# A written-out issue order for a two-layer graph network: scores and weighted sums on TensorE's row and column tiles, grouped differently

## The chip, the cores and the metric

One core of one Trainium2 chip runs the kernel. The metric is the device time of one execution in microseconds (us). TensorE (PE in the profile, PEld for its weight loads), VectorE (DVE), ScalarE (ACT) and GpSimd (POOL) each take their instructions in the order in which the program holds them; SyncE (SP) issues the DMA transfers. An instruction that depends on another engine waits on a semaphore, and everything queued behind it on its own engine waits too.

## The reference, cut to what matters

There are 64 graphs of 256 nodes with 256 features. Each goes through two layers; weights are shared by all graphs. All data are f32, `adj` is int32 (here 0 or 1). Head width is 32, and there are 8 heads.

```python
# layer 0
q = src @ Wq + bq; k = src @ Wk + bk                       # 8 heads of 32
attn = softmax(q @ k.T / sqrt(32))
out = sum over r of (attn * (adj == r)) @ (src @ Wv[r] + bv[r])
x = layernorm(src + out @ Wo + bo)
x = layernorm(x + gelu(x @ W1 + b1) @ W2 + b2)             # 1024 hidden
# layer 1
q, k, v = x @ Wq, x @ Wk, x @ Wv
e = q @ k.T; e = where(e >= 0, e, 0.2 * e)
h = softmax(where(adj > 0, e, -9e15)) @ v
y = layernorm(concat(layernorm(h), x) @ Wffn.T) + x
```

## The kernel before, in words

Everything of one graph is some 120 steps, written in the function `fast_path` as calls of `op(engine, reads, writes, emit)`. A step belongs to one engine and issues one to sixteen instructions. The 64 graphs overlap, like iterations of a software pipeline, and the order in which the steps of all graphs stand is written out by hand: `STARTS` gives each step of a graph a start, graph g is set off by `g * PERIOD`, and `in_order` sorts all steps of all graphs by that number. For the first four and the last four graphs a list of its own per graph (`FIRST`, `LAST`) takes the place of `STARTS`. The numbers serve as sort keys alone; nothing in the program waits for a time. Within an engine the sorted order is the order of execution.

```python
def in_order(programs, starts, period, first, last):
    ops = []
    for g, p in enumerate(programs):
        edge = first[g] if g < len(first) else last[g - len(programs)] if g >= len(programs) - len(last) else None
        at = edge or [starts[o.name] for o in p]
        ops += [(round(g * period + t, 3), o) for t, o in zip(at, p)]
    return [o for _, o in sorted(ops, key=lambda x: x[0])]
```

The names that follow are the keys of `STARTS`, in which the first digit is the layer, the second one is the group of four heads (hg 0 or 1), and `/0`, `/1` are the two pairs of heads of that group. `#2` and `#3` are the second and third step that write a tile.

- `pq0`, `pk0`, `pq1`, `pk1`, `pv1`, `pwo`, `pwa`, `pwb` are linear maps on TensorE, each four f32 matmuls of 128x128 weights by 256 columns (the trace shows two records for each, so x8); `pva0`, `pva1` are the two halves of layer 0's values; `py0`, `py1`, `ph` are transposes; `ph0`, `ph2`, `ph4`, `ph6` and `pw2` to `pw2#8` are the feed-forward part (32 + 32 records). All of these use the whole 128x128 array.
- `s00`, `s01`, `s10`, `s11` are the scores of four heads (`score`, L434). A head has only 32 rows to contract, so four heads lie beside one another on four row tiles (32x128) of the array; x16 records.
- `po00`, `po01`, `po10`, `po11` are the weighted sums (`weighted`, L470) and the row sums of the softmax (L475). A head has 32 output columns, so four heads lie on four column tiles (128x32). Layer 0 has parts `e`, `m` and `es` (x16, x16, x8 records), layer 1 has `e` and `es`.
- The scores of a group go to one PSUM tile `s` with room for one group alone (`TAGS`: "s" has one buffer), which is read pair by pair by two engines. In layer 0 ACT makes `e00/0` and `e00/1` of it (exp, L448) and DVE makes `m00/0` and `m00/1` (mask added, L457; ACT's exp `m00/0#2` follows in place). In layer 1 DVE makes `e10/0` and `e10/1` (mask added, L457) and ACT makes `m10/0` and `m10/1` (scaled relu, L706); POOL adds the two (`e10/0#2`, L710), and ACT takes the exp (`e10/0#3`). `es` is the sum of two halves on POOL (L501).
- `rd00` is DVE's reciprocal of the row sums (L484), `o0/0` and `o0/1` are the two products `po * rd` of layer 0 (L487), and `DVE:po00` is a check of the sums (L492). `pwo` multiplies by `o0/0` in its first matmul and by `o0/1` in its second one.
- `mv0` to `mv3` are the statistics of the four layer norms on DVE, `rs0` to `rs3` POOL's inverse roots, `y0`, `y1`, `y2` the normalised tiles; `q1`, `k1`, `v1`, `y0T`, `y1T` and `hT` are ACT's copies out of PSUM.

All tiles but `s` rotate through two to four buffers; PSUM's other tiles share one pool of four buffers ("g").

Of the kernel before, what the change touches and what calls it, by code (L numbers as in the profile page):

```python
# [44 lines left out]
def in_order(programs, starts, period, first, last):  # L45
# [4 lines left out]
    for g, p in enumerate(programs):  # L50
# [50 lines left out]
    "xT": 16.39, "x": 17.62, "pk0": 18.03, "adj": 19.67, "neg": 20.08, "pq0": 21.31, "k0": 22.13, "q0": 25.00,  # L101
    "s00": 31.15, "m00/1": 33.61, "e00/0": 37.30, "e00/1": 38.52, "m00/1#2": 39.34, "m00/0": 40.16, "s01": 40.57,
    "e01/0": 40.98, "e01/1": 41.39, "m00/0#2": 44.26, "pva0": 45.49, "es01/1": 46.31, "v0/0": 46.72, "pva1": 47.13,
    "v0/1": 48.36, "es00/0": 48.77, "es00/1": 50.82, "m01/0": 52.05, "m01/0#2": 52.87, "m01/1": 54.92,
    "es01/0": 55.33, "m01/1#2": 57.38, "po00": 57.79, "rd00": 58.20, "po01": 58.61, "o0/0": 60.25,
    "DVE:po01": 61.48, "rd01": 62.30, "o0/1": 62.70, "pwo": 63.11, "DVE:po00": 63.52, "res": 64.34, "pwo#2": 65.57,
    "mv0": 66.80, "rs0": 67.21, "y0": 69.26, "py0": 71.72, "y0T": 72.54, "ph6": 75.41, "ph0": 76.64, "hT/6": 77.87,
    "ph2": 78.69, "hT/2": 79.10, "ph4": 79.51, "hT/0": 79.92, "hT/4": 80.74, "pw2": 81.97, "pw2#2": 82.38,
    "r1": 82.79, "r1#2": 83.20, "pw2#3": 84.43, "pw2#4": 84.84, "pw2#5": 85.66, "pw2#6": 86.07, "pw2#7": 86.48,
    "pw2#8": 88.93, "pw2#9": 91.80, "mv1": 93.03, "rs1": 93.44, "y1": 94.67, "py1": 97.54, "y1T": 97.95,  # L110
    "pk1": 100.00, "ACT:adj": 100.41, "pq1": 104.10, "q1": 104.51, "k1": 109.02, "s10": 109.43, "m10/0": 109.84,
    "pv1": 110.66, "v1": 111.07, "x2": 111.89, "pwb": 113.93, "e10/0": 114.75, "e10/1": 115.16, "e10/0#2": 115.98,
    "m10/1": 118.44, "e10/1#2": 118.85, "e10/0#3": 120.49, "es10/0": 120.90, "zb": 122.95, "s11": 123.36,
    "e11/1": 123.77, "x2#2": 124.18, "e11/0": 124.59, "e10/1#3": 125.82, "es10/1": 126.23, "m11/0": 127.05,
    "m11/1": 127.46, "e11/1#2": 128.28, "e11/0#2": 130.33, "po10": 131.56, "rd10": 134.02, "o1/0": 135.25,
    "e11/1#3": 136.89, "e11/0#3": 137.70, "es11/0": 138.11, "es11/1": 139.75, "po11": 142.21, "DVE:po10": 142.62,
    "rd11": 143.85, "o1/1": 145.08, "DVE:po11": 145.90, "ph": 149.18, "pwa": 149.59, "mv2": 151.23, "rs2": 151.64,
    "pwa#2": 152.46, "mv3": 153.28, "rs3": 153.69, "y2": 155.74, "y2#2": 156.15, "y2#3": 156.56, "SP:y2": 156.97,
# [3 lines left out]
        -2847.053, -2618.669, -2552.639, -2604.994, -2706.544, -2524.281, -2429.355, -2491.963, -2326.15, -2291.878,  # L122
        -2205.017, -2453.681, -2501.433, -2475.116, -1979.242, -2495.418, -2281.166, -2149.469, -1954.32, -1950.672,
        -2629.93, -2490.837, -2900.007, -2402.608, -1755.256, -2397.873, -2429.046, -2408.233, -2387.015, -2337.739,
        -2248.383, -2096.592, -2381.743, -2040.963, -2323.494, -1986.344, -2170.731, -2048.634, -1860.558, -2191.888,
        -2201.038, -2121.273, -1987.509, -1858.163, -1687.597, -1539.069, -1758.675, -1901.191, -1868.775, -1849.204,
        -1797.723, -1842.922, -1866.564, -1901.189, -1864.039, -1710.05, -1635.372, -1608.525, -1601.055, -1611.923,
        -1504.663, -1503.313, -1503.311, -1454.211, -1453.749, -1428.651, -1397.418, -1365.689, -1263.132, -1333.428,
        -1307.057, -1302.867, -1269.069, -1279.736, -1246.049, -1318.829, -1287.58, -1268.965, -1234.872, -1196.915,
        -1176.186, -1166.684, -1155.815, -1135.153, -1127.66, -1127.658, -1125.664, -1116.163, -1109.387, -1096.892,  # L130
        -1068.525, -1058.771, -834.708, -1034.909, -1034.369, -1037.42, -971.802, -873.683, -861.526, -817.316,
        -794.117, -948.046, -931.884, -938.676, -839.591, -800.872, -786.885, -935.815, -938.986, -873.329, -822.37,
        -800.254, -703.594, -628.579, -521.145, -703.592, -852.402, -753.92, -797.646, -753.918, -687.087, -549.142,
        -801.786, -794.56, -679.67, -651.382, -613.255, -519.88, -503.788, -460.172, -508.16, -452.842, -406.466,
        -405.026, -445.465, -387.29, -386.804, -373.855, -368.241, -277.528, -258.371, -211.016,
    ],
    [
        -1712.66, -1443.453, -1558.578, -1409.383, -424.973, -1332.342, -1515.918, -1376.199, -1389.201, -1376.896,
        -1176.315, -1175.399, -1171.179, -1142.744, -1372.605, -1177.435, -1233.494, -1225.381, -1169.756, -1364.499,
        -1211.174, -1210.635, -1283.409, -1142.483, -1107.236, -1024.81, -1042.32, -1168.101, -1163.006, -1109.044,  # L140
        -1086.417, -1040.287, -1117.876, -1135.775, -1092.749, -1107.742, -1028.857, -1019.047, -1019.045, -962.29,
        -953.415, -933.383, -905.03, -894.712, -878.269, -878.267, -878.265, -878.267, -829.154, -849.496, -805.626,
        -860.667, -839.105, -834.236, -762.88, -849.583, -795.469, -753.483, -652.438, -623.714, -612.52, -604.112,
        -604.11, -604.108, -597.853, -597.851, -580.455, -541.025, -525.23, -510.162, -510.16, -234.294, 26.726,
        -461.818, -418.06, -444.927, -353.251, -347.025, -276.942, -284.894, -256.944, -353.249, -292.158, -353.247,
        -288.969, -272.27, -239.253, -352.105, -312.477, -253.791, -237.655, -177.565, -140.907, -63.211, -56.41,
        -132.185, -252.617, -248.041, -236.522, -133.806, -99.059, -66.449, -235.239, -211.498, -143.046, -63.735,
        -23.871, -15.497, 7.986, 8.437, -15.495, 28.391, 37.806, 44.002, 37.535, 66.321, 66.323, 87.244, 87.246,
        116.225, 189.089, 204.842,
    ],  # L150
    [
        -1229.881, -526.973, -1181.68, -1178.71, 66.635, -396.146, -1031.055, -966.68, -943.117, -935.039, -608.969,
        -560.147, -579.485, -523.949, -808.47, -704.853, -753.672, -752.036, -617.846, -650.977, -671.842, -631.081,
        -641.14, -494.019, -442.274, -439.507, -456.199, -629.154, -609.944, -493.554, -466.947, -559.795, -577.488,
        -482.336, -418.455, -494.253, -414.141, -410.734, -406.722, -370.63, -396.854, -333.908, -310.914, -309.856,
        -309.854, -305.407, -305.13, -200.379, -114.553, -302.188, -284.917, -285.604, -156.698, -263.97, -217.918,
        -280.388, -230.946, -154.247, -111.16, -83.43, -79.414, -74.774, -71.445, -70.202, -70.114, -67.694, -67.692,
        -67.69, -53.693, -53.691, -53.689, -24.507, 209.443, 29.562, 64.838, -35.526, 9.223, 71.488, 99.662, 113.468,
        120.616, 69.818, 89.502, 70.022, 89.536, 110.394, 124.527, 109.105, 79.783, 120.842, 123.12, 124.465, 131.394,
        133.646, 137.555, 133.656, 123.327, 128.611, 127.875, 129.152, 133.924, 133.926, 123.329, 127.217, 128.709,  # L160
        133.424, 138.627, 142.388, 142.522, 146.364, 145.361, 151.44, 151.442, 153.783, 152.66, 153.785, 153.787,
        155.037, 155.83, 196.784, 209.445, 209.447,
    ],
    [
        -394.579, -455.288, -369.201, -318.002, -85.508, -1.925, -382.842, -372.891, -372.581, -353.322, -106.738,
        -80.656, -102.13, -71.463, -265.115, -179.435, -120.231, -102.022, -128.718, -168.609, -153.486, -32.837,
        -58.709, -10.119, 11.78, 27.092, 37.379, -119.809, -73.356, -86.43, -39.705, -50.805, -93.331, -55.921,
        -14.902, -55.763, 4.094, 33.398, 33.4, 47.121, 58.796, 65.314, 65.316, 67.626, 72.399, 72.484, 72.486, 72.401,
        78.893, 74.741, 81.291, 76.79, 81.396, 75.033, 81.051, 79.917, 81.961, 83.124, 83.126, 84.564, 85.156, 88.277,
# [898 lines left out]
```

## Time and profile before

| | us |
|---|---|
| median of 3 runs | 2936.52 |
| lowest and highest | 2935.5, 2936.69 |
| the profiled execution's own time | 2934.98 |
| its span in the profile | 2932.8 |
| PE busy in the span | 2882.9 (98%) |
| PE's granted clock, mean | 0.995 |
| DVE, ACT, POOL busy | 1961.4 (67%), 1788.6 (61%), 2017.2 (69%) |

The profiled execution took 2.2 us more than its span, and 1.5 us less than the median of the runs. Times in the timeline are microseconds from the start of the span: the first column is the start of a group of like instructions, the second one is its length up to the end of the last of them. As matmuls overlap, what a group costs TensorE is read as the distance from its start to the start of the next group. A remark in brackets at the end of a line is idle time of that engine before the group, and who ended it.

### The profile page before, as it was taken

How to read it: one execution, taken by the hardware profiler on the slowest of the kernel's cores; microseconds unless marked ns; L12 is line 12 of the kernel's file. 1: busy time of each engine (PE TensorE's matmuls, PEld its weight loads, DVE VectorE, ACT ScalarE, POOL GpSimd, SP SyncE). 2: the span in 40 equal slices, each digit the busy share in tenths (PEclk: the TensorE clock that was granted, in tenths of full speed). 3: DMA queues.
4: the chain of work that ended last, by engine and by line, in shares of the span. 5: the costliest groups of instructions: out<-in, count | busy, mean ns of one | idle time of the engine just before them, and what ended most of it. 6: DMA issues, size and time to landing. Idle time of an engine off the chain costs nothing.

```text
span 2932.8 us, 53746 instructions
## 1 busy us (share of the span) xinstructions
PE 2882.9 (98%) x21770; PEld 2154.7 (73%) x21770; DVE 1961.4 (67%) x3668; ACT 1788.6 (61%) x3009; POOL 2017.2 (69%) x1542
## 2 busy tenths in 40 slices
PE   7999999999999999999999999999999999999996
PEld 5777777777777777777777777777777777777774
DVE  4676676676766766766767667667667676676674
ACT  4656656566566566566665665665666656656653
POOL 2657767767767667677667676676776676766666
PEclk9999999999999999999999999999999999999997
DMA  3000100000000000000000000000000000010000
GB/s 123 15 19 16 33 30 15 30 19 26 30 15 30 30 15 30 30 15 30 21 24 30 16 30 30 16 30 30 15 30 23 23 30 16 30 34 15 30 16 8
DMA packets 74331, 76.65 MB, mean 26 GB/s; under 512 B 4448, under 2 KB 73568, under 8 KB 74080
## 3 DMA queue, kind: packets, MB, share of 16 engines
q1 hardware_dynamic: 74080, 73.17, 7.8%
q8 instruction: 174, 2.85, 0.4%
q14 instruction: 77, 0.63, 0.1%
HBM read 56.37 MB, written 16.78 MB: 25 GB/s over the span
## 4 chain that ended last, share of the span: by engine, by line
PE 96%; DVE 1%; POOL 1%; ACT 1%; issue 1%; DMA 0%; SPq 0%; DVEq 0%; ACTq 0%; POOLq 0%
PE ph L658 15%; PE pw L676 15%; PE po L470 12%; PE s L434 9%; PE pva L610 8%; PE pq L338 8%; PE pk L338 7%; PE pv L352 4%; PE pwa L352 4%; PE po L475 4%; PE pwo L352 4%; PE pwb L352 4%; PE py L364 2%; PE ph L364 1%; POOL e L710 1%
## 5 line engine op out<-in xcount | busy, mean ns | idle before, releaser
L710 POOL TENSOR_TENSOR e<-e,m 128x1024 f32<-128x1024 f32 x256 | 601.3, 2359 | 231.7 <-DVE e L457 148.8
L501 POOL TENSOR_TENSOR es<-e 128x512 f32<-128x512 f32 x512 | 644.4, 1274 | 153.1 <-ACT e L448 143.1
L457 DVE TENSOR_TENSOR m<-s,neg 128x1024 f32<-128x1024 f32 x256 | 311.8, 1219 | 483.8 <-PE s L434 327.7
L484 DVE RECIPROCAL rd<-po 128x256 f32<-128x256 f32 x256 | 449.2, 1755 | 132.1 <-PE po L475 124.5
L410 POOL TENSOR_TENSOR rs<-ve,neg_half 128x2 f32<-128x2 f32 x256 | 178.5, 697 | 479.6 <-DVE ve L405 479.3
L706 ACT ACTIVATE m<-s 128x1024 f32<-128x1024 f32 x256 | 255.2, 1022 | 371.2 <-PE s L434 226.1
L658 PE MATMUL ph<-y0T,w 128*128 128x256 f32 x2048 | 459.2, 382 | 0.7 <-ACT y0T L380 0.7
L676 PE MATMUL pw<-w,hT 128*128 128x256 f32 x2048 | 459.0, 382 | 0.0
L676 PEld LDWEIGHTS pw<-w,hT 128*128 128x128 f32 x2048 | 383.9, 190 | 75.6 <-issue 25.1
L658 PEld LDWEIGHTS ph<-y0T,w 128*128 128x128 f32 x2048 | 383.8, 190 | 71.2 <-issue 20.6
L457 DVE TENSOR_TENSOR e<-s,neg 128x1024 f32<-128x1024 f32 x256 | 302.1, 1218 | 146.8 <-PE s L434 122.9
L448 ACT ACTIVATE e<-s 128x1024 f32<-128x1024 f32 x256 | 258.9, 1014 | 187.4 <-PE s L434 167.1
L448 ACT ACTIVATE m<-m 128x1024 f32<-128x1024 f32 x256 | 269.5, 1055 | 66.8 <-DVE m L457 66.8
L434 PE MATMUL s<-q,k 32*128 32x256 f32 x4096 | 293.3, 400 | 3.1 <-DVE e L457 1.4
L448 ACT ACTIVATE e<-e 128x1024 f32<-128x1024 f32 x256 | 270.4, 1056 | 27.1 <-POOL e L710 26.2
L470 PE MATMUL po<-e,v 128*32 128x256 f32 x4096 | 276.4, 385 | 4.3 <-ACT e L448 4.3
L434 PEld LDWEIGHTS s<-q,k 32*128 32x128 f32 x4096 | 185.1, 184 | 89.9 <-issue 78.7
L610 PE MATMUL pva<-wv,xT 128*128 128x512 f32 x512 | 237.0, 605 | 0.0
L470 PEld LDWEIGHTS po<-e,v 128*32 128x32 f32 x4096 | 114.1, 109 | 125.5 <-issue 45.4
L665 ACT ACTIVATE hT<-ph,cols 128x256 f32<-128x256 f32 x512 | 194.6, 488 | 3.4 <-PE ph L658 2.6
L610 PEld LDWEIGHTS pva<-wv,xT 128*128 128x128 f32 x512 | 92.1, 189 | 115.7 <-issue 115.4
L475 PE MATMUL po<-es,ones 128*32 128x256 f32 x2048 | 160.2, 381 | 4.0 <-POOL es L501 4.0
(90 smaller groups left out, 4546.5 us busy)
## 6 DMA issues: line engine op xcount, KB each, us to landing
adj<-adjT_dram SPq DMA_DIRECT2D x64, 256.0 KB, 3.6
xT<-xT_dram SPq DMA_DIRECT2D x64, 256.0 KB, 3.0
x<-x_dram SPq DMA_DIRECT2D x64, 256.0 KB, 3.1
out_dram<-y SPq DMA_DIRECT2D x64, 256.0 KB, 2.2
w<-L_gnn_W_dram SPq DMA_DIRECT2D x2, 1024.0 KB, 10.3
rows<-rows_dram SPq DMA_DIRECT2D x1, 896.0 KB, 7.4
wv<-L_gnn_Wv_dram SPq DMA_DIRECT2D x3, 256.0 KB, 7.2
wq<-L_gnn_Wq_dram SPq DMA_DIRECT2D x2, 256.0 KB, 5.9
```

The source lines that it names most:

```text
L338: nc.tensor.matmul(pt[:, o, :], lhsT=w[:, c, o * P : (o + 1) * P], rhs=s[:, c, :], start=(c == 0), stop=(c == KC - 1),)
L352: nc.tensor.matmul(pt[:, t, :], lhsT=T(s)[:, c, t * P : (t + 1) * P], rhs=w, start=(n == 0), stop=(n == len(parts) - 1),)
L434: nc.tensor.matmul(s[:, j, c, :], lhsT=kT[r, hg, c * P : (c + 1) * P], rhs=qT[r, hg, :], start=True, stop=True,)
L448: nc.scalar.activation(T(dst)[:, j], T(src)[:, j], AF.Exp, scale=scale, **kw)
L457: lambda: nc.vector.tensor_tensor(T(dst)[:, j], T(src)[:, j], T("neg")[:, None].to_broadcast([P, 2, NT, D]), ALU.add),
L470: nc.tensor.matmul(po[j * DH : (j + 1) * DH, 0, :], lhsT=v(c, j), rhs=T(e)[:, j, c, :], start=(n == 0 and c == 0), stop=(n == len(parts) - ...
L484: op("DVE", [po], [f"{rd}:rd"], lambda: nc.vector.reciprocal(T(rd), T(po)[:, 1, :]))
L501: lambda: on.tensor_tensor(T(dst)[:, j], T(e)[:, j, 0, :], T(e)[:, j, 1, :], ALU.add),
L610: nc.tensor.matmul(pv.rearrange("p r d -> p (r d)"), lhsT=s[:, c, t * P : (t + 1) * P], rhs=wv0[:, c].rearrange("p r d -> p (r d)"), start ...
L658: nc.tensor.matmul(ph[:, i, :], lhsT=w1[:, c, (f + i) * P : (f + i + 1) * P], rhs=s[:, c, :], start=(c == 0), stop=(c == KC - 1),)
L676: nc.tensor.matmul(T("pw2")[:, t, :], lhsT=T("hT")[:, f + i, t * P : (t + 1) * P], rhs=w2[:, f + i, :], start=(f + i == 0), stop=(f + i == ...
L710: nc.gpsimd.tensor_tensor(T(f"e1{hg}")[:, j], T(f"e1{hg}")[:, j], T(f"m1{hg}")[:, j], ALU.add)
```

## The change

Only the numbers in `STARTS`, `FIRST` and `LAST` are others; the steps, what each of them computes, the tiles, their buffers and `PERIOD` are the same. By the built programs, in the steady state, TensorE's order for one graph's worth of work was this (a visit to row or column tiles in brackets; graph numbers left out):

```
before: pk1 pq1 [po00 po01 s10] pv1 pwo pwb pk0 pq0 py0 [s11] ph x4 [s00 po10] pw2 [s01 po11] pva0 pva1 py1 ph pwa
after:  py1 pva1 pk1 ph pq1 pva0 [s10 po00 po01 s11] pv1 pwo pk0 pq0 pwa py0 [s00] ph x4 pw2 pwb [s01 po10 po11]
```

In its own words the change makes three visits instead of five; the built orders hold three instead of four.

The steps of the other engines are put in another order as well. After `s10` the order is, on DVE, `e10/0, e10/1, rd00, o0/0, DVE:po01, rd01, o0/1, DVE:po00, e11/1, e11/0, pwo#2`, and on ACT `m10/0, m10/1, e10/0#3, v1`. Before, it was `rd00, o0/0, DVE:po01, rd01, o0/1, DVE:po00, e10/0, e10/1, pwo#2` on DVE and `m10/0, v1, m10/1, e10/0#3` on ACT. A graph's first step (a load) and its last (the store) are 196 apart on the clock of `STARTS` where they were 141. The three loads of a graph come in another order on SP, and so do the weights ahead of the first graph: the first transfers were `adj`, `wq0`, `rows0`, `xT`, `wk0`, and are `wk0`, `xT`, `cols`, `wv01`, `wq0`.

The diff, with the lists of `FIRST` and `LAST` cut to a sample:

```diff
@@ STARTS @@
 PERIOD = 50.00
 STARTS = {
-    "xT": 16.39, "x": 17.62, "pk0": 18.03, "adj": 19.67, "neg": 20.08, "pq0": 21.31, "k0": 22.13, "q0": 25.00,
-    "s00": 31.15, "m00/1": 33.61, "e00/0": 37.30, "e00/1": 38.52, "m00/1#2": 39.34, "m00/0": 40.16, "s01": 40.57,
-    "e01/0": 40.98, "e01/1": 41.39, "m00/0#2": 44.26, "pva0": 45.49, "es01/1": 46.31, "v0/0": 46.72, "pva1": 47.13,
-    "v0/1": 48.36, "es00/0": 48.77, "es00/1": 50.82, "m01/0": 52.05, "m01/0#2": 52.87, "m01/1": 54.92,
-    "es01/0": 55.33, "m01/1#2": 57.38, "po00": 57.79, "rd00": 58.20, "po01": 58.61, "o0/0": 60.25,
-    "DVE:po01": 61.48, "rd01": 62.30, "o0/1": 62.70, "pwo": 63.11, "DVE:po00": 63.52, "res": 64.34, "pwo#2": 65.57,
-    "mv0": 66.80, "rs0": 67.21, "y0": 69.26, "py0": 71.72, "y0T": 72.54, "ph6": 75.41, "ph0": 76.64, "hT/6": 77.87,
-    "ph2": 78.69, "hT/2": 79.10, "ph4": 79.51, "hT/0": 79.92, "hT/4": 80.74, "pw2": 81.97, "pw2#2": 82.38,
-    "r1": 82.79, "r1#2": 83.20, "pw2#3": 84.43, "pw2#4": 84.84, "pw2#5": 85.66, "pw2#6": 86.07, "pw2#7": 86.48,
-    "pw2#8": 88.93, "pw2#9": 91.80, "mv1": 93.03, "rs1": 93.44, "y1": 94.67, "py1": 97.54, "y1T": 97.95,
-    "pk1": 100.00, "ACT:adj": 100.41, "pq1": 104.10, "q1": 104.51, "k1": 109.02, "s10": 109.43, "m10/0": 109.84,
-    "pv1": 110.66, "v1": 111.07, "x2": 111.89, "pwb": 113.93, "e10/0": 114.75, "e10/1": 115.16, "e10/0#2": 115.98,
-    "m10/1": 118.44, "e10/1#2": 118.85, "e10/0#3": 120.49, "es10/0": 120.90, "zb": 122.95, "s11": 123.36,
-    "e11/1": 123.77, "x2#2": 124.18, "e11/0": 124.59, "e10/1#3": 125.82, "es10/1": 126.23, "m11/0": 127.05,
-    "m11/1": 127.46, "e11/1#2": 128.28, "e11/0#2": 130.33, "po10": 131.56, "rd10": 134.02, "o1/0": 135.25,
-    "e11/1#3": 136.89, "e11/0#3": 137.70, "es11/0": 138.11, "es11/1": 139.75, "po11": 142.21, "DVE:po10": 142.62,
-    "rd11": 143.85, "o1/1": 145.08, "DVE:po11": 145.90, "ph": 149.18, "pwa": 149.59, "mv2": 151.23, "rs2": 151.64,
-    "pwa#2": 152.46, "mv3": 153.28, "rs3": 153.69, "y2": 155.74, "y2#2": 156.15, "y2#3": 156.56, "SP:y2": 156.97,
+    "adj": 38.52, "xT": 38.93, "pva0": 63.52, "v0/0": 63.93, "neg": 64.75, "pk0": 76.23, "pq0": 77.05, "q0": 78.69,
+    "k0": 80.33, "ACT:adj": 85.25, "s00": 85.66, "e00/0": 86.07, "e00/1": 86.48, "m00/1": 86.89, "x": 88.11,
+    "m00/0": 89.75, "res": 96.72, "m00/0#2": 97.54, "s01": 98.36, "es00/1": 102.87, "pva1": 105.74,
+    "m00/1#2": 106.56, "v0/1": 107.79, "e01/1": 108.20, "es01/1": 108.61, "e01/0": 109.43, "m01/1": 109.84,
+    "m01/1#2": 110.25, "m01/0": 111.48, "es01/0": 112.70, "es00/0": 114.34, "m01/0#2": 115.16, "po00": 117.62,
+    "rd00": 118.03, "o0/0": 118.44, "po01": 119.67, "DVE:po01": 120.08, "rd01": 120.49, "o0/1": 120.90,
+    "DVE:po00": 122.54, "pwo": 124.18, "pwo#2": 125.41, "mv0": 125.82, "rs0": 126.64, "y0": 129.10, "r1": 129.51,
+    "r1#2": 129.92, "py0": 131.15, "y0T": 131.56, "ph0": 137.70, "ph2": 140.16, "hT/0": 140.57, "ph4": 140.98,
+    "hT/4": 141.39, "hT/2": 141.80, "ph6": 142.21, "hT/6": 142.62, "pw2": 143.44, "pw2#2": 143.85, "pw2#3": 144.26,
+    "pw2#4": 144.67, "pw2#5": 145.08, "pw2#6": 145.49, "pw2#7": 145.90, "pw2#8": 147.13, "pw2#9": 148.77,
+    "mv1": 149.59, "rs1": 151.64, "y1": 152.05, "py1": 152.46, "y1T": 154.92, "pk1": 159.02, "k1": 161.07,
+    "pq1": 161.89, "q1": 162.30, "s10": 165.57, "e10/0": 165.98, "m10/0": 166.39, "e10/1": 166.80, "m10/1": 167.21,
+    "e10/0#2": 169.26, "s11": 171.31, "e10/0#3": 171.72, "es10/0": 172.13, "e11/1": 172.95, "pv1": 173.36,
+    "v1": 173.77, "e11/0": 174.59, "e10/1#2": 175.00, "m11/1": 177.46, "m11/0": 177.87, "e11/1#2": 178.28,
+    "e11/1#3": 184.02, "e11/0#2": 187.30, "es11/1": 189.34, "e10/1#3": 193.03, "es10/1": 196.31, "pwb": 197.95,
+    "po10": 199.18, "e11/0#3": 200.00, "es11/0": 200.41, "po11": 200.82, "zb": 201.23, "rd10": 203.28,
+    "o1/0": 203.69, "x2": 204.10, "x2#2": 204.51, "DVE:po10": 205.33, "rd11": 206.15, "o1/1": 206.97,
+    "DVE:po11": 207.38, "ph": 210.66, "mv2": 213.11, "rs2": 218.85, "pwa": 230.74, "pwa#2": 231.97, "mv3": 232.38,
+    "rs3": 232.79, "y2": 233.20, "y2#2": 233.61, "y2#3": 234.43, "SP:y2": 234.84,
 }
@@ FIRST, four lists: the first list's first lines @@
 FIRST = [
     [
-        -2847.053, -2618.669, -2552.639, -2604.994, -2706.544, -2524.281, -2429.355, -2491.963, -2326.15, -2291.878,
-        -2205.017, -2453.681, -2501.433, -2475.116, -1979.242, -2495.418, -2281.166, -2149.469, -1954.32, -1950.672,
...
+        -4869.342, -5664.963, -5275.464, -4917.328, -4768.579, -4238.972, -4026.569, -2961.223, -4179.356, -4393.785,
+        -4053.676, -4275.361, -4753.625, -4403.686, -2182.272, -3651.889, -3597.415, -3402.061, -3183.955, -3105.665,
...
```

## Prediction

> **What bounds the kernel now.** I read the page's busy times first, then the stretches of one graph's length, then TensorE's timeline.
>
> ```profile
> PE 2882.9 (98%) x21770; PEld 2154.7 (73%) x21770; DVE 1961.4 (67%) x3668; ACT 1788.6 (61%) x3009; POOL 2017.2 (69%) x1542
> ...
> PE 96%; DVE 1%; POOL 1%; ACT 1%; issue 1%; DMA 0%; SPq 0%; DVEq 0%; ACTq 0%; POOLq 0%
> ```
>
> TensorE is never idle but at the ends. Of the 49.9 us of the span in which it is (2932.8 - 2882.9), two lie between 100 and 2700 us. The stretches of busy time show one graph in the middle:
>
> ```profile
> 999.93:1044.72 44.79, 44.79 (x342) 33.58 (x341) 30.51 (x57) 27.93 (x47) 31.54 (x24) 1.00 0.08 25
> ```
>
> 44.79 us a graph, all of it TensorE (second number), at the full clock (1.00). 64 x 44.79 is 2866.6, so the ends cost 66 us. DVE, ACT and POOL have a third of their time free, but each works in order, and what counts is when a particular step is done. TensorE's timeline shows what a visit to row or column tiles costs:
>
> ```profile
> 1008.58 1.89 PE L338 MATMUL pk<-y1T,wk 128*128 128x256 f32 x8
> 1010.31 1.89 PE L338 MATMUL pq<-y1T,wq 128*128 128x256 f32 x8
> 1012.13 1.07 PE L470 MATMUL po<-e,v 128*32 128x256 f32 x16
> 1013.02 1.05 PE L470 MATMUL po<-m,v 128*32 128x256 f32 x16
> 1013.88 0.61 PE L475 MATMUL po<-es,ones 128*32 128x256 f32 x8
> 1014.31 1.05 PE L470 MATMUL po<-e,v 128*32 128x256 f32 x16
> 1015.17 1.05 PE L470 MATMUL po<-m,v 128*32 128x256 f32 x16
> 1016.04 0.61 PE L475 MATMUL po<-es,ones 128*32 128x256 f32 x8
> 1016.58 1.15 PE L434 MATMUL s<-q,k 32*128 32x256 f32 x16
> 1017.66 1.99 PE L352 MATMUL pv<-wv,y1T 128*128 128x256 f32 x8
> 1019.49 1.89 PE L352 MATMUL pwo<-wo,o 128*128 128x256 f32 x8
> ```
>
> From start to start: a linear map takes 1.73 (pk), but 1.82 ahead of a visit (pq) and 1.83 behind one (pv). Within one kind of tile x16 records take 0.86 and x8 take 0.43. `es` ahead of a change of tiles takes 0.54; scores, which always border on changes, take 1.08.
>
> **What the saved visit is worth.** Each visit against the same groups at 0.86 and 0.43. [po00 po01 s10]: 1012.13 to 1017.66 is 5.53, less 5.16, plus 0.10 on either neighbour, makes 0.57. [s11] alone: 1.08 - 0.86 + 0.20 = 0.42. [s00 po10] and [s01 po11]: scores 1.08, `e` 0.89, `es` 0.54 is 2.51, less 2.15, plus 0.20, makes 0.56 each. Sum before: 2.11. After: [s10 po00 po01 s11] is 1.08 + (0.89 + 0.86 + 0.43) + (0.86 + 0.86 + 0.54) + 1.08 = 6.60, less 6.02, plus 0.20, makes 0.78. [s00] 0.42. [s01 po10 po11] is 1.08 + 1.32 + 1.40 = 3.80, less 3.44, plus 0.20, makes 0.56. Sum after: 1.76. The change saves 0.35 us a graph, if TensorE stays fed: 44.44 instead of 44.79.
>
> **What it puts in the way.** There is one `s` tile. `s11` may start only when both readers of `s10` are done, and the built order makes them take turns: `e10/0` on DVE, then `m10/0` on ACT waits for it, then `e10/1` on DVE waits for that, then `m10/1` on ACT, and `s11` waits for `m10/1`. Before, 10.3 us of TensorE's work lay between `s10` and `s11` (1016.58 to 1026.93); now only `po00` and `po01` do. Such turns show in this trace:
>
> ```profile
> 1014.56 1.76 DVE L484 RECIPROCAL rd<-po 128x256 f32<-128x256 f32 x1 [1.04 <-PE po L475]
> 1016.36 0.42 DVE L487 TENSOR_TENSOR o<-po,rd 128x256 f32<-128x256 f32 x1
> 1016.72 0.42 DVE L492 TENSOR_REDUCE flags<-po 128x1 f32<-128x256 f32 x1
> 1017.06 1.75 DVE L484 RECIPROCAL rd<-po 128x256 f32<-128x256 f32 x1
> 1018.85 0.42 DVE L487 TENSOR_TENSOR o<-po,rd 128x256 f32<-128x256 f32 x1
> 1019.18 0.41 DVE L492 TENSOR_REDUCE flags<-po 128x1 f32<-128x256 f32 x1
> 1019.52 2.35 DVE L457 TENSOR_TENSOR e<-s,neg 128x1024 f32<-128x1024 f32 x2
> ```
>
> ```profile
> 1017.86 1.02 ACT L706 ACTIVATE m<-s 128x1024 f32<-128x1024 f32 x1 [3.60 <-PE s L434]
> ...
> 1021.90 1.02 ACT L706 ACTIVATE m<-s 128x1024 f32<-128x1024 f32 x1 [1.62 <-DVE e L457]
> ```
>
> ACT's second `m` waited 1.62 us, until 0.03 after DVE's `e` pair had ended (1019.52 + 2.35 = 1021.87). The first reader starts 1.28 after the scores do (1016.58 to 1017.86).
>
> Now the new order, in us from the start of `s10`. Two clocks run.
>
> TensorE, if fed: `po00` 1.08, `po01` 3.26, `s11` due 5.52, `pv1` 6.60, `pwo` 8.43, its second matmul (the one that reads `o0/1`) 0.43 later, due 8.86.
>
> The readers: `e10/0` 1.28 to 2.50 (1.22 each), `m10/0` 2.53 to 3.55 (1.02 each), `e10/1` 3.58 to 4.80, `m10/1` 4.83 to 5.85. The 0.03 from ACT to DVE is that of `m00/0` (1042.39 to 1042.42); from ACT to TensorE it is 0.06 (near the end a copy of q ended at 2893.94 and the scores began at 2894.00). So `s11` starts at 5.91: 0.39 late.
>
> DVE does both `e` steps ahead of the reciprocals, where before they came behind. `rd00` starts at 4.71 (a DVE group's next one starts 1.13 after an `e`). From the lines above, `rd` to `o` is 1.80, `o` to the check 0.36, check to `rd` 0.34, `rd` to `o` 1.79: `o0/0` 6.51, `DVE:po01` 6.87, `rd01` 7.21, `o0/1` 9.00, done at 9.42. The second matmul of `pwo` starts at 9.48. As `s11` was 0.39 late it had been due at 9.25 by then, so 0.23 more is lost. Together 0.62 us against 8.86. Queued behind that matmul on TensorE is everything else, and nothing there has slack to give back.
>
> Sum a graph: -0.35 + 0.62 = +0.27.
>
> **Moves that I cost at nothing, and what hides them.** `s10` itself needs `q1`: from the start of `py1`, ACT does `y1T`, `m00/1#2`, `e01/1`, `e01/0`, then waits for DVE's `m01/1`, then `m01/1#2`, `k1`, `q1`: 0.64 + 0.91 + 0.96 + 1.01 + 1.10 + 0.03 + 1.22 + 0.03 + 0.96 + 0.48 + 0.58 + 0.06 = 7.98, beside TensorE's 0.53 + 1.72 + 1.73 + 0.43 + 1.73 + 1.82 = 7.96. A tie: nothing if it holds, up to 0.2 a graph if ACT comes late. `py0` needs `y0`, which is done 3.70 after `pwo#2` starts (1021.78 to 1025.48 before). DVE gets there by way of `DVE:po00` 9.33, `e11/1` 9.67, `e11/0` 10.80, at 11.93; 15.63, due about 15.9. `s00` is due about 16.5; `m11/0` ends by 14.1 and `k0` by 16.0. The waits `s00` to `s01` and `s01` to `s10` have over 10 us of TensorE's work each, against 4.5 of reading. The other layer norms and POOL's steps are 1.5 us or more ahead of their users. SP's store now stands ahead of the next loads; these are issued some 18 us before first use and land in 3.0 to 3.6.
>
> **The ends.** Their 66 us are weight loads, the first graph's chain and the last one's. The first TensorE step needs `xT` and `wq0`. Before, the later of the two was `xT`, issued at 2.23, and TensorE began at 8.85; now it is `wq0`, behind `wk0`, `xT`, `cols` and two of `wv01`, whose issues took 0.47, 0.43, 0.92 and 0.98, so at about 3.6: some 1.3 later. Between `pwo` and the first `py0` stand three groups where one did, which takes away the 1.8 us of idle there. The last graph's chain from `s10` to the store is the same. I take the ends as unchanged, and put 5 us either way into the range.
>
> The wait recurs from graph 0 to graph 61; I count 60 of them. 60 x 0.27 = 16. The profiled execution's own time is 2935.0, so it becomes 2951; the median of the runs lies 1.5 above it, so 2953.
>
> **A rule that would turn this.** In the trace DVE's `m00/0` (1042.42) waited 2.46 us for ACT, which was reading the other pair, `e00/1`, from 1041.29 on; its own pair had been free since 1040.35. So the turns span pairs here. The Trainium skill, page "PSUM — Partial Sum Buffer", section "PSUM bank collisions raise a hardware error", asks only that two engines keep off the same bank, and its banks of 2 KiB put the two pairs of an 8 KiB tile in different ones. By the page `e10/1` would follow `e10/0` at once, neither wait would arise, and the sum would be the first rival's.
>
> **The rivals.** (1) Faster: the visit is saved and no wait replaces it: 2936.5 - 60 x 0.35 = 2915. It decides if `o0/1` is done within 8.80 of `s10`'s start. For it: DVE and ACT are a third idle. Against it: the order of DVE's queue alone (`rd00` behind both `e`). Chance 0.08. (2) No change: only `s11`'s 0.39 is lost, `pwo` is not, or a part of 0.62: +0.04 x 60 = 2, 2939. It needs handoffs or steps shorter by 0.2 than their rows. Chance 0.10. (3) My forecast, 2953. Chance 0.60. (4) Slower still: the tie at `q1` breaks, or the handoffs over which I count 0.03 are the 0.12 that others in this trace take (`m11/0` after `e11/0`); 0.2 to 0.3 a graph more, 2965 to 2971. Chance 0.15. (5) The ends: graphs stay in flight 196 instead of 141 of the order's clock; if filling and draining grow as much, the 48 us that TensorE idles in the first 100 and the last 233 us become 67, 2972 with the wait. Against it: TensorE's work there is only moved. Chance 0.07. That the change does less than it says (five visits to three) is in the sum: built, it is four to three.
>
> What this kernel's measurement can tell from no change is about 0.2%, 5.9 us. Faster than 2930.6 is rival 1: 0.08. Within is rival 2 and a little of the low side of mine: 0.12. Slower takes the rest, 0.80. For 8 times in 10 the range leaves out rival 1 and the far ends of 4 and 5: 2938 to 2968.
>
> **What would show it.** Right: a graph in the middle takes 45.0 to 45.1 us; TensorE's waits list `s` L434 <- ACT `m` L706 at 0.3 to 0.5, and `pwo` L352 <- DVE `o` L487 at 0.2, some 60 times each; idle time of TensorE near 85 us instead of 50. Wrong: a graph at 44.4 with neither wait, or waits of TensorE on another step.

## The result and the profile after

| | before | after |
|---|---|---|
| median of 6 runs, us | 2936.61 | 2955.32 |
| lowest and highest, us | 2935.31, 2937.55 | 2954.78, 2955.66 |
| ratio, with its 95% interval | | 1.0064 [1.0051, 1.0077] |
| span of the profiled execution, us | 2932.8 | 2953.4 |
| one graph in the middle, us | 44.79 | 45.14 |

The changed kernel is slower by 18.7 us. In the page its engines look as they did:

```profile
PE 2886.5 (98%) x21770; PEld 2161.0 (73%) x21770; DVE 1979.9 (67%) x3668; ACT 1783.2 (60%) x3013; POOL 2016.3 (68%) x1542
...
PE 79%; ACT 11%; DVE 8%; issue 1%; POOL 1%; DMA 0%; SPq 0%; DVEq 0%; ACTq 0%; POOLq 0%
```

The second line is the chain that ended last, by engine. TensorE's share of it was 96% and is 79%; ACT and DVE have the 19% that went through their steps. The windows of busy time say where in the run that is. From the left: stretch, its length, then busy us and records of PE, PEld, DVE, ACT and POOL, the granted clock, the DMA share, GB/s.

```profile
100.00:2700.00 2600.00, 2579.78 (x19623) 1935.03 (x19622) 1780.96 (x3292) 1594.59 (x2700) 1811.23 (x1381) 1.00 0.08 24
...
1015.60:1060.74 45.14, 44.81 (x341) 33.64 (x341) 30.84 (x58) 27.72 (x48) 31.52 (x25) 1.00 0.08 24
```

Between 100 and 2700 us TensorE now idles 20.2 us where it idled 2 before. One graph, from one `s10` to the next, takes 45.14, of which 0.33 is listed as idle. TensorE's timeline from `pva0` to `pk0`, to be read against the five groups `po` to `pwo` of before:

```profile
1013.67 1.88 PE L615 MATMUL pva<-wv,xT 128*128 128x512 f32 x4
1015.60 1.15 PE L439 MATMUL s<-q,k 32*128 32x256 f32 x16
...
1021.46 1.15 PE L439 MATMUL s<-q,k 32*128 32x256 f32 x16 [0.26 <-ACT m L711]
1022.53 1.99 PE L357 MATMUL pv<-wv,y1T 128*128 128x256 f32 x8
1024.37 2.18 PE L357 MATMUL pwo<-wo,o 128*128 128x256 f32 x8
1026.38 1.89 PE L343 MATMUL pk<-xT,wk 128*128 128x256 f32 x8
```

Three places lose time. `s11` starts 5.86 after `s10` where 5.52 or 5.53 was due: 0.33. From `pwo` to `pk0` pass 2.01 (1026.38 - 1024.37) where a `pwo` took 1.73: 0.28. From `pva0` to `s10` pass 1.93 where a map ahead of a visit takes 1.82: 0.11. Only the first carries a remark. DVE's and ACT's timelines, here put one behind the other, show what `s11` and `pwo` wait for:

```profile
1016.81 1.22 DVE L462 TENSOR_TENSOR e<-s,neg 128x1024 f32<-128x1024 f32 x1 [0.51 <-PE s L439]
1019.12 1.22 DVE L462 TENSOR_TENSOR e<-s,neg 128x1024 f32<-128x1024 f32 x1 [1.09 <-ACT m L711]
1020.27 1.75 DVE L489 RECIPROCAL rd<-po 128x256 f32<-128x256 f32 x1
...
1024.50 0.43 DVE L492 TENSOR_TENSOR o<-po,rd 128x256 f32<-128x256 f32 x1
```

```profile
1014.96 0.59 ACT L511 COPY q<-pq 128x512 f32<-128x512 f32 x1
...
1018.07 1.02 ACT L711 ACTIVATE m<-s 128x1024 f32<-128x1024 f32 x1 [1.57 <-DVE e L462]
...
1020.38 1.02 ACT L711 ACTIVATE m<-s 128x1024 f32<-128x1024 f32 x1 [1.29 <-DVE e L462]
```

The four readers of `s10` take turns, `e`, `m`, `e`, `m`, each starting 0.03 or 0.04 after the end of the one before; the last one ends at 1021.40 and `s11` starts at 1021.46. `o0/1` ends at 1024.93. The second matmul of `pwo` loads it as weights. Its first record was due at 1024.80 (0.43 after the start of `pwo`); it starts at 1024.98, together with its weight load (PEld), and is 0.48 long, where the median of `pwo`'s records is 0.38. So 0.18 late and 0.10 longer make the 0.28:

```profile
1024.98 0.48 PE L357 MATMUL pwo<-wo,o 128*128 128x256 f32 x1
1024.98 0.30 PEld L357 LDWEIGHTS pwo<-wo,o 128*128 128x128 f32 x2 [0.42 <-DVE o L492]
```

ACT's copy of `q1` ends at 1015.55, and `s10` starts 0.05 later: the third wait.

TensorE's waits, as the profile lists them (us in total, times, the longest in us), first of its matmuls, then of its weight loads:

```profile
PE s L439 <- ACT m L711: 17.1, 61, 1.3
...
PE pwo L357 <- DVE o L492: 3.7, 4, 2.2
```

```profile
PEld pwo L357 <- DVE o L492: 29.7, 62, 2.6
```

### The profile page after: what moved, and what is told of

Its sections match the earlier page's. It is cut to its first block, busy times and chain, and to the rows that moved or that the text cites. A ratio compares the mean times of both kernels' runs of the same rounds, so it can differ in the third digit from the quotient of the medians.

```text
span 2953.4 us, 53562 instructions
## 1 busy us (share of the span) xinstructions
PE 2886.5 (98%) x21770; PEld 2161.0 (73%) x21770; DVE 1979.9 (67%) x3668; ACT 1783.2 (60%) x3013; POOL 2016.3 (68%) x1542
## 4 chain that ended last, share of the span: by engine, by line
PE 79%; ACT 11%; DVE 8%; issue 1%; POOL 1%; DMA 0%; SPq 0%; DVEq 0%; ACTq 0%; POOLq 0%
PE ph L663 15%; PE pw L681 15%; PE s L439 10%; PE pq L343 6%; PE pk L343 6%; DVE e L462 5%; ACT m L711 4%; PE pwo L357 4%; PE po L475 4%; PE pv L357 4%; PE pva L615 4%; PE pwb L357 4%; PE pwa L357 4%; ACT e L453 2%; PE py L369 2%; ACT m L453 2%
## 5 line engine op out<-in xcount | busy, mean ns | idle before, releaser
L681 PE MATMUL pw<-w,hT 128*128 128x256 f32 x2048 | 452.8, 379 | 0.0
L663 PEld LDWEIGHTS ph<-y0T,w 128*128 128x128 f32 x2048 | 385.4, 191 | 72.3 <-issue 20.6
L397 DVE TENSOR_TENSOR pw<-pw,r 128x512 f32<-128x512 f32 x64 | 44.8, 700 | 491.4 <-PE pw L681 491.4
L462 DVE TENSOR_TENSOR m<-s,neg 128x1024 f32<-128x1024 f32 x256 | 302.2, 1220 | 80.1 <-ACT e L453 60.2
L385 ACT ACTIVATE y1T<-py,cols 128x256 f32<-128x256 f32 x128 | 65.2, 560 | 453.1 <-PE py L369 453.0
L439 PE MATMUL s<-q,k 32*128 32x256 f32 x4096 | 294.7, 402 | 29.2 <-ACT m L711 17.1
L453 ACT ACTIVATE e<-e 128x1024 f32<-128x1024 f32 x256 | 269.3, 1052 | 19.4 <-POOL e L715 18.7
L475 PEld LDWEIGHTS po<-e,v 128*32 128x32 f32 x4096 | 120.2, 110 | 111.4 <-issue 44.2
```

Source lines behind the costliest of these rows:

```text
L439: nc.tensor.matmul(s[:, j, c, :], lhsT=kT[r, hg, c * P : (c + 1) * P], rhs=qT[r, hg, :], start=True, stop=True,)
L453: nc.scalar.activation(T(dst)[:, j], T(src)[:, j], AF.Exp, scale=scale, **kw)
L462: lambda: nc.vector.tensor_tensor(T(dst)[:, j], T(src)[:, j], T("neg")[:, None].to_broadcast([P, 2, NT, D]), ALU.add),
L475: nc.tensor.matmul(po[j * DH : (j + 1) * DH, 0, :], lhsT=v(c, j), rhs=T(e)[:, j, c, :], start=(n == 0 and c == 0), stop=(n == len(parts) - ...
L663: nc.tensor.matmul(ph[:, i, :], lhsT=w1[:, c, (f + i) * P : (f + i + 1) * P], rhs=s[:, c, :], start=(c == 0), stop=(c == KC - 1),)
L681: nc.tensor.matmul(T("pw2")[:, t, :], lhsT=T("hT")[:, f + i, t * P : (t + 1) * P], rhs=w2[:, f + i, :], start=(f + i == 0), stop=(f + i == ...
```

## The experiments

My theory: the turns over the one `s` tile hold up `s11` and `pwo`, 0.62 us a graph together; the copy of `q1` holds up `s10`, 0.11; without them the order would save what the fewer visits are worth. The rivals: the order lengthens TensorE's own work, or the ends of the run; or banks of PSUM, not the tile, set the turns. All edits below are on the changed kernel, but for one that says otherwise. The "graph" of a result is the distance of like groups in the middle of its trace.

**Turns by pairs.** `m10/0` is put behind `e10/1`, so that DVE does both its steps, and then ACT does both of its own. The number of handoffs falls from three to one.

```diff
-"e10/0": 165.98, "m10/0": 166.39, "e10/1": 166.80, "m10/1": 167.21
+"e10/0": 165.98, "e10/1": 166.80, "m10/0": 166.82, "m10/1": 167.21
```

> The changed kernel with one number moved: in the middle graphs m10/0 stands behind e10/1, so DVE reads both pairs of s10, then ACT reads both. The visits, and all else, stay. Theory (the turns of the readers of s10 and DVE's queue behind them): e10/0 1.28 to 2.50, e10/1 2.41 to 3.63, m10/0 3.66, m10/1 ends 5.64, s11 at 5.70 instead of 5.86, so its wait goes from 0.33 to 0.17 us; rd00 starts at 3.54 instead of 4.71, o0/1 is done at 8.31, and the 0.28 at pwo goes. 0.44 us a graph on 56 graphs is 25 us: 2931. Rival A (the loss is a price of the new visit itself, or of deeper overlap, not of the readers' order): nothing changes, 2955. Rival B (only the wait listed for s11 costs): 0.16 x 56 = 9 us, 2946.

Measured: 2928.16 us, 0.9972 [0.9961, 0.9982] of before; the graph 44.64. TensorE's timeline:

```profile
1010.05 1.15 PE L439 MATMUL s<-q,k 32*128 32x256 f32 x16
...
1015.71 1.15 PE L439 MATMUL s<-q,k 32*128 32x256 f32 x16
...
1018.62 1.89 PE L357 MATMUL pwo<-wo,o 128*128 128x256 f32 x8
1020.34 1.03 PE L343 MATMUL pk<-xT,wk 128*128 128x256 f32 x4
```

`pwo` to `pk0` is 1.72 again, and `s11` comes 5.66 after `s10`: 0.13 late instead of 0.33, and not listed. One number in the order turns the change from slower to faster, with the same visits. It took 27.2 us off where 0.50 x 60 = 30 would follow from the graph. Between the two profiled executions it is 25.1: 28.1 less from the first `pv` to the last one, but the first one came 2.9 later (83.54 for 80.66), as the start of the run went slower; there TensorE waited 9.8 for its first load instead of 8.4.

**ACT first.** Both `m10` are put ahead of both `e10`. There is one handoff too, but now DVE's steps, and the reciprocals behind them, are late.

```diff
-"e10/0": 165.98, "m10/0": 166.39, "e10/1": 166.80, "m10/1": 167.21
+"m10/0": 165.92, "m10/1": 165.94, "e10/0": 165.98, "e10/1": 166.80
```

> The changed kernel with m10/0 and m10/1 ahead of both e10 steps in the middle graphs: ACT reads both pairs of s10, then DVE does. Theory: e10/1 ends at 5.63, so s11 starts at 5.78, about where it did; but rd00 comes behind e10/1, at 5.54 instead of 4.71, so o0/1 is done at 10.25 and the second matmul of pwo at 10.3 instead of 9.48: 0.8 us a graph more, 56 x 0.8 = 45 us, 3000. Rival B (only the wait for s11 costs): same as the changed kernel, 2955 or a little less. Rival A: 2955.

Measured: 2998.47 us, 1.0213 [1.0197, 1.0228]; the graph 45.93. TensorE's timeline and its first wait:

```profile
1037.04 0.59 PE L357 MATMUL pwo<-wo,o 128*128 128x256 f32 x2
1038.62 1.56 PE L357 MATMUL pwo<-wo,o 128*128 128x256 f32 x6 [0.98 <-DVE o L492]
1040.02 1.89 PE L343 MATMUL pk<-xT,wk 128*128 128x256 f32 x8
```

```profile
PE pwo L357 <- DVE o L492: 57.6, 58, 2.2
```

The wait of `pwo` is the long form of the 0.28 above, in the same place: ahead of the second matmul. From `pwo` to `pk0` pass 2.98, 1.25 more than 1.73; 0.98 of it is listed. The rest is 0.16 by which the first two records run past the time at which the third was due (1037.63 for 1037.47), and 0.10 by which the third is longer, 0.48 again. So when DVE's `rd` and `o` come free sets TensorE's time directly, and a listed wait is less than what it costs.

**q1 early.** ACT's exp `m01/1#2`, which stood ahead of `k1` and `q1`, is put behind them.

```diff
-"m01/1#2": 110.25
+"m01/1#2": 112.35
```

> The changed kernel with ACT's m01/1#2 behind q1 instead of ahead of k1 in the middle graphs. Theory: the 0.11 us that s10 starts later than its neighbours' prices allow (1.93 from pva0 to s10, where an edge costs 1.82) is its wait for q1, the tie of the prediction that broke. Without it 0.11 x 56 = 6 us less, 2949. Rival (the 0.11 is part of the price of going to row tiles behind pva0): 2955.

Measured: 2946.93 us, 1.0041 [1.0027, 1.0055]; the graph 45.03. TensorE's timeline:

```profile
1010.82 1.88 PE L615 MATMUL pva<-wv,xT 128*128 128x512 f32 x4
1012.63 1.15 PE L439 MATMUL s<-q,k 32*128 32x256 f32 x16
...
1018.49 1.15 PE L439 MATMUL s<-q,k 32*128 32x256 f32 x16 [0.26 <-ACT m L711]
```

`pva0` to `s10` is 1.81 where it was 1.93, and the wait of `s11` stays. The graph lost 0.11, as the trace had it, which is 7 us over 60 graphs; the time fell by 8.4, and the runs of this kernel are up to 4 us apart.

**Both edits**, turns by pairs and `q1` early.

> The two moves that helped the changed kernel together, without the split: m10/0 behind e10/1, and m01/1#2 behind q1. Theory: the waits lie one behind the other on TensorE, so the gains add: 2928 less 8 (what the second move gave by itself) is 2920, and of the recurring waits only some 0.15 at s11 is left. Rival (the second move's gain is the same time as the first one's): 2928.

Measured: 2921.03 us, 0.9949 [0.9935, 0.9962]; the graph 44.54. The two gains nearly add (27.2 and 8.4 alone, 34.3 together), as separate waits do. `s11` still comes 5.66 after `s10`, 0.13 late.

**Two score tiles.** The order of the change stays as it is. The tile `s` of four heads becomes two of two heads each, `sa` and `sb`, in the same 8 KiB of a partition; each reader names the tile of its pair.

```diff
-    "s": ([HPG, NT, D], F32, 1),
+    "sa": ([2, NT, D], F32, 1),
+    "sb": ([2, NT, D], F32, 1),
...
-                                s[:, j, c, :], lhsT=kT[r, hg, c * P : (c + 1) * P], rhs=qT[r, hg, :],
+                                s[j // 2][:, j % 2, c, :], lhsT=kT[r, hg, c * P : (c + 1) * P], rhs=qT[r, hg, :],
```

> The changed kernel with the score tile made two tiles of two heads each, in the same four banks. The steps and their order stay; a reader of one pair no longer has to take turns with a reader of the other pair. Theory: e10/1 follows e10/0 at once (2.41 to 3.63), m10/1 ends at 4.68, s11 is due at 5.53 and starts then; rd00 at 3.54, o0/1 done at 8.31, no wait at pwo; m01/1 no longer waits for e01/0, so q1 is 0.2 early and s10 starts on time. All three waits go, 0.33 + 0.28 + 0.11 on 60 graphs, 43 us: 2912, and a graph takes 44.4 us. Rival A: 2955. Rival C (TensorE is held by something else as soon as these are gone, such as py0 or hT): between 2915 and 2940, with waits at another step.

Measured: 2895.11 us, 0.986 [0.9845, 0.9875]; the graph 44.41. DVE's and ACT's timelines, one behind the other:

```profile
1040.74 1.22 DVE L467 TENSOR_TENSOR e<-s10a,neg 128x1024 f32<-128x1024 f32 x1 [0.38 <-PE s10b L441]
1041.88 1.21 DVE L467 TENSOR_TENSOR e<-s10b,neg 128x1024 f32<-128x1024 f32 x1
```

```profile
1041.99 1.03 ACT L716 ACTIVATE m<-s10a 128x1024 f32<-128x1024 f32 x1 [1.77 <-DVE e L467]
```

DVE goes on to the second pair at once, and ACT reads the first pair beside it (1041.99 to 1043.02 within 1041.88 to 1043.09); both steps take what they took alone, 1.21 and 1.03. So it was the tile, not the banks, that set the turns between the pairs. Within a pair the turns remain: ACT's wait of 1.77 ends 0.03 after `e10/0`. TensorE, in the windows:

```profile
100.00:2700.00 2600.00, 2600.00 (x19922) 1976.91 (x19921) 1810.06 (x3346) 1628.90 (x2750) 1842.86 (x1403) 1.00 0.08 25
```

No idle time is left, and no wait hides in the distances between groups: `pwo` to `pk0` is 1.73 (1047.99 to 1049.72), `s10` to `s11` 5.53 (1039.56 to 1045.09), and the graph is within 0.03 of the 44.44 that the prediction added up without waits. The new order's own TensorE work takes 44.41 a graph, so the rival that it lengthens that work falls. The 0.73 to 45.14 were waits that the one tile caused; that at `q1` is among them (`pva0` to `s10` is 1.81 here, 1037.75 to 1039.56), though `q1` itself was not moved. The kernel is 17 us faster than I expected: 64 x 44.41 is 2842, and the span of 2893.0 leaves 51 for the ends, where the changed kernel has 64 (2953.4 - 64 x 45.14). Of these 13, 11.4 lie between the last two `pv`: 51.55 in the changed kernel (from 2872.87), 40.11 here (from 2820.51). There TensorE idled 8.7 and idles 2.2, as its waits for `py` behind DVE's `y` (3.25) and for `s` behind DVE's `e` (2.81) and ACT's `m` (1.29) went or shrank to 0.45 and less. And it was busy 42.9 with 241 records where it now takes 37.9 for 240, at a mean granted clock of 0.87 then and 1.00 now. The other kernels with the new order and one tile take 47.9 to 51.5 for the stretch, the one of the last experiment, with two tiles, 40.11. Why less clock was granted was not tested.

**The same two tiles in the kernel before.**

> The kernel before, in its own order, with the score tile made two tiles as in the split kernel. Theory: in its middle TensorE is never idle, so a graph stays at 44.79 us and only the first and last graphs can gain: 2925 to 2936. The split order then beats it by the price of the saved visit, 0.35 x 60 = 21 us, plus or minus the ends. Rival D (splitting the tile is worth some 40 us to any order, so the new order has no part in the gain): about 2895.

Measured: 2926.36 us, 0.9964 [0.9951, 0.9978]; the graph 44.79 as before. So the split is worth nothing in the middle of the old order, where 10.3 us lie between `s10` and `s11`, and 8 (spans) to 10 us (medians) at its ends. With two tiles in both, the new order is 31.3 us ahead (2926.36 - 2895.11), of which (44.79 - 44.41) x 60 = 23 is TensorE's shorter work in the middle; the other 8 lie at the ends.

**Four visits again.** In the kernel with two tiles, `s11` is moved out of its visit, behind `pv1`; `e11/1` follows it.

```diff
-"s11": 171.31, "e11/1": 172.95
+"s11": 173.50, "e11/1": 173.60
```

> The split kernel with s11 moved behind pv1 in the middle graphs (and e11/1 on DVE behind it), so that TensorE makes four visits again: [s10 po00 po01] pv1 [s11] pwo. No wait is near, so this measures what a visit costs by itself. Theory: the visits' prices are 0.56 and 0.42 instead of 0.78, so 0.20 us a graph, 56 x 0.20 = 11 us: 2906, and a graph takes 44.6 us. Rival E (the visits are free and the split alone made the gain): 2895.

Measured: 2905.65 us, 0.9896 [0.9881, 0.9911]; the graph 44.60. One visit more costs 0.19 to 0.20 a graph: by the rows of the prediction [s10 po00 po01] and [s11] apart are 0.57 + 0.42, together 0.78, so 0.21. TensorE is busy throughout in both. So half of the 0.38 is the visit of `s11`. The other half (44.79 to 44.60) lies between two orders with four visits each. The rows put 0.14 on it: [s00 po10] and [s01 po11] at 0.56 each became [s00] at 0.42 and [s01 po10 po11] at 0.56. No run here takes that part by itself.

## Why the prediction held, step by step

- **Forecast.** 2953 for a measured 2955.3, by the mechanism named. The graph was put at 45.06 (44.79 + 0.27) and is 45.14.
- **The saved visit, 0.35.** With the waits out of the way the graph is 44.41, 0.38 below the old one; 44.44 was expected. Shown by the two split kernels.
- **The wait of `s11`, 0.39, and of `pwo`, 0.23.** Measured 0.33 and 0.28, together the expected 0.62 within 0.01. That it is so near is luck. The first reader started 1.21 after `s10`, not 1.28, and the whole chain came earlier with it: `s11` started at 5.86 instead of 5.91, and `o0/1` was done at 9.33 instead of 9.42. With the prediction's 0.06 from there to the matmul, the loss would have been 9.39 - 8.86 = 0.53. The matmul did start at 9.38, but its first record was 0.10 longer than its like, a term that the sum did not have. The two misses of about 0.1 cancelled; the mechanism, turns and then DVE's queue, is the one that the prediction named.
- **The tie at `q1`, costed at nothing.** This is the term that was off in the total: 0.11 a graph, 7 us. ACT's side took 8.03 instead of 7.98, as `y1T` came 0.69 after `py1` where the row of before had 0.64; TensorE's side would have taken 7.92 instead of 7.96, as `py1` took 0.49 and not 0.53. The prediction named the place and "up to 0.2", but took zero, though its own sum had ACT 0.02 late and its rows scatter by 0.05; half of the upper price would have been nearer. It is the first half of rival 4, at about half the price given there. The second half, handoffs of 0.12, did not come: they took 0.03 and 0.04.
- **The ends.** Taken as unchanged. By 64 graphs they went from 66.6 to 64.4: 2 us less, where rival 5 had 19 more. Of the prediction's terms for them, the idle 1.8 ahead of the first `py0` did go, but TensorE did not begin 1.3 later: it began at 8.39, 0.46 earlier than before. In the seven kernels with the new order it began at 7.6 to 9.8, so 2 us are about what the start alone scatters by. With the missed 7 this makes the sum: 64 x (45.14 - 44.785) = 22.7, less 2.2, is the 20.6 between the spans. The medians are 18.7 apart, as the profiled execution of before lay further below its median than that of after.
- **The list of waits.** Right for `s11`: 56 times 0.26 between 100 and 2700 us (14.7 of the listed 17.1), near the 0.3 to 0.5. Wrong for `pwo`, listed 4 times among the matmuls and not 60, and for TensorE's idle time, 66.9 instead of about 85. The wait at `pwo` is there 62 times, but in the list of the weight loads. A matmul's record runs past the time at which the next one was due: the second record of `pwo` ends at 1024.96, 0.02 ahead of the third, which is 0.18 late. So the wait shows as a longer group, 2.18 instead of 1.89. In a graph 0.40 of the 0.73 counts as busy (44.81 - 44.41).
- **Rival 1** (2915, no wait in place of the visit) needed pairs in different banks to be free of each other, as the Trainium skill's "PSUM — Partial Sum Buffer" has it, section "PSUM bank collisions raise a hardware error". Both are true of this case: the chip let DVE and ACT read the two pairs side by side, at 1.21 and 1.03, once they were two tiles; with one tile of four banks the program's own waits kept them apart (DVE's second `e` waited 1.09 for ACT's `m` of the other pair). The page tells what the chip allows, the trace what the program asked for.

## What to carry to other kernels

Before two steps that depend on one tile are moved nearer to each other, add up the readers' turns from the first step's start, handoff by handoff, and set them against the work that is left between. Where such turns are in the way, a tile that two engines read half by half is better two tiles: the halves then wait for nothing but their own. Where they are not, as in the middle of the old order, splitting the tile was worth nothing. When two chains come out equal, do not price the one that may be late at zero (here half its worst was near, in one case); and measure TensorE's loss by the distance between the starts of like groups, not by its idle time.

## What I had not expected

- TensorE's busy share is 98% before and after, while the graph is 0.35 longer: 0.40 us of waiting in a graph is counted as busy. In the kernel where `pwo` waited longest, 0.98 is listed of 1.25 lost.
- Handoffs of 0.03 us are not what the turns cost. With three of them the four readers end 5.80 after `s10` (1021.40), with one they end at 5.61 (1013.72 + 1.94 - 1010.05). What the edit by pairs moved was DVE, which is free for the reciprocals at 3.57 instead of 4.74 after `s10`; that took away the 0.28 at `pwo`.
- The ends of the run shrank with two tiles by 13 us in the new order and 8 to 10 in the old one. In the new order most of it is one stretch near the end, where TensorE waits less and is granted more clock; in the old one the place is open.
